# Issuing the late stores of a gated block-sparse and LoRA kernel from GpSimd's DMA queue instead of ScalarE's

## The chip, the cores and the metric

The kernel runs on one core of one Trainium2 chip. The metric is device time in microseconds (us), the median of several runs; lower is better.

## The reference

The input `x` has two batches of 1024 tokens with 1024 features. Every token is layer-normalised. Two products of 1024 by 1024 are taken of the result and combined with the input:

```
xn = layernorm(x)
s  = xn @ (weight masked in 32x32 blocks).T + bias
c  = softmax(((mean of xn over tokens) @ Wq.T) @ keys.T / sqrt(128))    # 8 numbers per batch
W  = W_org + sum over e of c[e] * lora_down[e] @ lora_up[e]             # folded, per batch
out = x + s * silu(xn @ W.T)
```

The kernel uses that the LoRA branch is linear: it folds the eight experts into one weight matrix per batch, which needs the coefficients `c` of that batch first. Everything is float32; each operand of a product is split into a high part (`fp32r`) and a low rest, and each product is three matmuls (high-high, high-low, low-high).

## The kernel before

**Stages.** Batch 0 is computed tile by tile: 128 tokens by 512 output columns per PSUM tile, 24 matmuls each (`gemm`, lines 425 to 427). The stages that matter here, with their place in the profiled span:

- about 100 to 155 us, `jobs_b`: the y product of batch 0 for the first 512 columns. Each tile's result is finished by `final_evac` in a tile `res` and queued for storing. Beside it the statistics of batch 1 are taken (GpSimd computes eight `rstd` by a power, line 152).
- about 155 to 206 us, `jobs_c`: the y product for the other 512 columns. Beside it VectorE normalises batch 1 in transposed form and forms, for each of four slices `j`, seven token sums (`wide_a`, `wide_b`, the operands of a seven-product scheme for batch 1), which are queued for storing in a DRAM tile `xv` (five stores for each j: `ac`, `bd`, and three single tiles). At the end the coefficients of batch 1 are computed: scores on TensorE (line 332), a few small VectorE operations (L334 to L337), the exponential `ex` on GpSimd (L339), the softmax's rest on VectorE (L345 to L352), and `scale_up` scales `up` by them (ScalarE L367, VectorE L368) into four tiles `cut`.
- about 204 to 300 us, the folding: sixteen calls of `fold`, one for each piece of 128 rows by 512 columns of batch 1's folded weight, between the eight tiles of batch 0's last product (`s_tile`). They come in bursts of 4, 4, 3, 3 and 2 folds. A fold loads `ds` and `wo`, splits `ds` into `dhi` and `dlo` (L380, L381), runs 12 matmuls (L389 to L391) with `cut`, adds `wo` (L396) and queues the sum for storing in a DRAM tile `yu`. After eight folds `scale_up(1, 1)` loads the other half of `up` (tiles `us`) and scales it for the last eight.
- from about 306 us, batch 1's seven products (L1127), which read `xv` and `yu` back. They store their results from SyncE and are not touched.

**Queued stores.** Late stores aren't issued where their data is produced. They are appended to a list, and `store_late` issues what has gathered there at fixed points of the program. There are 52 in all: 16 of batch 0's results (256 KB each), 20 of `xv` (8 of 512 KB and 12 of 256 KB), 16 of `yu` (256 KB each, in DRAM pieces of 512 bytes).

**Order.** TensorE, VectorE, ScalarE and GpSimd run in the order of the program (`manual_schedule`). The order on SyncE, which issues all the loads, is chosen by a planner that simulates the program. A store's instruction waits, in its engine's queue, until its data is there, and what stands behind it in that queue waits too.

**Buffers.** `ds`, `wo`, `us` and others take turns in one pool of six buffers (tag `st`), so that a load can wait for an earlier store of the same buffer to land. In the program, the third and the fourth load of `us` for the second half are in buffers that the stores of fold 5 and fold 6 (counted from 0) must leave first.

**Descriptors.** The program is built with a small area for descriptors that GpSimd would write: `dynamic_dma_scratch_size=SCRATCH`, and `SCRATCH = 1024` (bytes of each partition).

Of the kernel before, what the change touches and what calls it, by code (L numbers as in the profile page):

```python
# [32 lines left out]
def kernel(  # L33
# [26 lines left out]
    nc = tc.nc  # L60
# [414 lines left out]
    late_stores = []  # L475

    def store_late():

        while late_stores:
            nc.scalar.dma_start(*late_stores.pop(0))  # L480

    pending = []

# [119 lines left out]
    with tc.manual_schedule(engines={mybir.EngineType.PE, mybir.EngineType.DVE, mybir.EngineType.Activation, mybir.EngineType.Pool}):  # L603
# [233 lines left out]
        def jobs_b(i):  # L837
            if i == 0:
                yield J(scale_up, 0, 1)
            yield J(mix_jobs, y01, 0, 1, i)  # L840
            yield J(store_late)
            if i < 4:
                yield J(mask_part, 2 + i // 2, i % 2)
            for t in ((0,), (1, 2), (3, 4), (5,), (6, 7), (), (), ())[i]:
                yield J(nat_stats, 1, t)
            if i == 4:
                yield J(wide_load, 0, 0)
                yield J(wide_load, 0, 1)
            if i == 5:
                yield J(spread_stats)  # L850
                yield J(wide_a, 0)
            if i == 6:
                yield J(wide_b, 0)
            if i == 7:
                yield J(wide_load, 1, 0)
                yield J(wide_load, 1, 1)
# [76 lines left out]
        def jobs_c(i):  # L933
            yield J(s_mul, s1, 1, i)
            yield J(store_late)
            yield J(s_lo, s1, 1, i)
            if i in (1, 3):
                yield J(wide_load, (i + 3) // 2, 0)
                yield J(wide_load, (i + 3) // 2, 1)
            if i < 6:  # L940
                yield J((wide_a, wide_b)[i % 2], 1 + i // 2)
            if i == 6:
                yield steps[0]
                yield steps[1]
            if i == 7:
                yield steps[2]
                yield steps[3]
                yield J(scale_up, 1, 0)
# [6 lines left out]
        def fold(n):  # L955
            h, kt = folds[n]
            if n + 1 < len(folds):
                y_prep(1, *folds[n + 1])
            store_late()
            y_mul(1, h, kt)  # L960
            flush()
            y_sum(1, h, kt)
            ps, ws = staged.pop((1, h, kt))
            late_stores.append((
                yu[:, :, 2 * h + kt // 4, kt % 4, :].rearrange("u p n -> p u n"),
                ws.rearrange("p (u n) -> p u n", n=P),
            ))
            if n == NKT - 1:
                scale_up(1, 1)
# [297 lines left out]
```

## Time and profile before

| what | value |
|---|---|
| median of 3 runs | 461.96 us (461.96 to 462.08) |
| profiled execution | 463.29 us, span 461.2 us |
| TensorE busy | 443.0 us, 96% of the span, 2047 matmuls |
| VectorE, ScalarE, GpSimd busy | 313.0, 169.3, 37.9 us |
| SyncE's queue (q1) | 73.42 MB, 49.1% of the 16 DMA engines |
| ScalarE's queue (q10) | 15.73 MB, 10.1% |
| GpSimd's queue | no DMA in this profile |

All times below come from the one profiled execution, whose own time of 463.29 us is 1.33 us above the median. The span is what its records cover. "Idle before" and "releaser" say how long an engine stood still ahead of an instruction and which instruction ended that wait. The records of DMA-issuing instructions stand on a row of their own for each engine's queue (ACTq for ScalarE, SPq for SyncE); they aren't counted as busy, but the engine's later instructions come after them.

### The profile page before, as it was taken

Reading aid. Unit: us, or ns where it says so; the run is one execution under the profiler, and the core shown is the slowest. Engines: PE = TensorE matmul, PEld = TensorE weight load, DVE = VectorE, ACT = ScalarE, POOL = GpSimd, SP = SyncE. Lnnn points to the kernel's source line nnn. Section 1 sums busy time; section 2 is a strip of 40 time slices with the busy share of each in tenths; the row PEclk is TensorE's granted clock in tenths of the full one; section 3 lists DMA queues with packets and bytes.
Section 4 is the critical chain, followed back from the end, with each engine's and each line's share of the span. In section 5 each row is a group of like instructions: output and inputs, shape, how many; then the busy total and the mean of one; then the engine's idle time right before and its main releaser. Section 6 shows DMA issues by size and latency. Waiting matters only on the chain.

```text
span 461.2 us, 5714 instructions
## 1 busy us (share of the span) xinstructions
PE 443.0 (96%) x2047; PEld 362.6 (79%) x2047; DVE 313.0 (68%) x504; ACT 169.3 (37%) x277; POOL 37.9 (8%) x40
## 2 busy tenths in 40 slices
PE   7799999999999999996999899999999999999996
PEld 5689888888887888874887688877888888888884
DVE  6989877667775788846555776769496196467624
ACT  4676534363223222214224223158343432441510
POOL 3884210000100000001000000000000000000000
PEclk9999999999999999998999999999999999999999
DMA  8996317687952688797887985664264134207003
GB/s 286 391 343 212 114 42 231 179 274 258 294 207 92 199 316 287 257 299 235 256 248 250 279 278 159 222 192 156 85 171 141 54 120 155 91 28 223 23 1 114
DMA packets 48172, 89.52 MB, mean 194 GB/s; under 512 B 4752, under 2 KB 14992, under 8 KB 48144
## 3 DMA queue, kind: packets, MB, share of 16 engines
q1 hardware_dynamic: 34512, 73.42, 49.1%
q10 hardware_dynamic: 13632, 15.73, 10.1%
q8 instruction: 16, 0.26, 0.2%
q14 instruction: 12, 0.10, 0.1%
HBM read 69.21 MB, written 19.92 MB: 193 GB/s over the span
## 4 chain that ended last, share of the span: by engine, by line
PE 74%; DVE 11%; DMA 10%; ACT 3%; issue 2%; SPq 0%; DVEq 0%; ACTq 0%
PE acc_ps L1127 22%; PE py L1127 9%; PE acc_ps L425 8%; PE acc_ps L427 8%; PE acc_ps L426 8%; PE psw L391 6%; PE psw L389 6%; PE psw L390 6%; DMA ws<-in_wT_dram 3%; DMA xv<-bd 2%; DMA xs<-xv 2%; DVE slot L544 1%; DMA raw<-in_x_dram 1%; DMA yu<-wo 1%; DMA us<-in_up_dram 1%
## 5 line engine op out<-in xcount | busy, mean ns | idle before, releaser
L1127 PE MATMUL acc_ps<-xw,ow 128*128 128x512 f32 x480 | 113.8, 393 | 0.7 <-ACT acc_ps L1158 0.4
L426 PE MATMUL acc_ps<-slot,xgrp 128*128 128x512 f32 (+1 forms) x288 | 105.8, 367 | 2.7 <-DVE slot L544 2.7
L1127 PEld LDWEIGHTS acc_ps<-xw,ow 128*128 128x128 f32 x480 | 90.0, 188 | 21.7 <-ACT acc_ps L1158 0.8
L425 PE MATMUL acc_ps<-slot,xgrp 128*128 128x512 f32 (+1 forms) x288 | 106.6, 370 | 0.1
L427 PE MATMUL acc_ps<-slot,xgrp 128*128 128x512 f32 (+1 forms) x288 | 105.6, 367 | 0.7 <-DVE xgrp L556 0.7
L426 PEld LDWEIGHTS acc_ps<-slot,xgrp 128*128 128x128 f32 x288 | 54.3, 189 | 12.2 <-DVE slot L544 3.6
L427 PEld LDWEIGHTS acc_ps<-slot,xgrp 128*128 128x128 f32 x288 | 54.2, 188 | 10.2 <-DVE xgrp L556 1.1
L425 PEld LDWEIGHTS acc_ps<-slot,xgrp 128*128 128x128 f32 x288 | 54.3, 188 | 9.1 <-DVE stash L439 0.3
L389 PE MATMUL psw<-cut,dhi 128*128 128x512 f32 x128 | 50.9, 398 | 4.5 <-ACT dhi L380 4.3
L391 PE MATMUL psw<-cut,dlo 128*128 128x512 f32 x128 | 50.9, 398 | 1.6 <-DVE dlo L381 1.5
L390 PE MATMUL psw<-cut,dhi 128*128 128x512 f32 x128 | 50.6, 395 | 0.0
L1127 PE MATMUL py<-xw,ow 128*128 128x512 f32 x192 | 46.9, 392 | 0.0
L1127 PEld LDWEIGHTS py<-xw,ow 128*128 128x128 f32 x192 | 36.1, 188 | 8.1
L1031 DVE TENSOR_TENSOR ow<-raw,ow 128x1024 fp32r<-128x1024 f32 (+1 forms) x32 | 34.5, 1089 | 11.2 <-ACT ow L1030 11.2
L380 ACT CAST dhi<-ds 128x512 fp32r<-128x512 f32 x32 | 19.8, 618 | 43.1 <-PE psw L390 24.3
L396 DVE TENSOR_TENSOR wo<-wo,psw 128x512 f32<-128x512 f32 x32 | 22.0, 686 | 17.3 <-PE psw L391 17.2
L389 PEld LDWEIGHTS psw<-cut,dhi 128*128 128x128 f32 x128 | 24.3, 190 | 10.2 <-ACT dhi L380 4.7
L391 PEld LDWEIGHTS psw<-cut,dlo 128*128 128x128 f32 x128 | 24.4, 191 | 8.4 <-DVE dlo L381 3.2
L1030 ACT CAST ow<-raw 128x1024 fp32r<-128x1024 f32 (+1 forms) x32 | 29.3, 939 | 2.0 <-DVE xw L986 2.0
L390 PEld LDWEIGHTS psw<-cut,dhi 128*128 128x128 f32 x128 | 24.3, 190 | 5.7 <-DVE cut L368 0.5
L381 DVE TENSOR_TENSOR dlo<-ds,dhi 128x512 fp32r<-128x512 f32 x32 | 21.9, 686 | 8.0 <-ACT dhi L380 8.0
L1172 DVE TENSOR_TENSOR py<-py,s 128x512 f32<-128x512 f32 x8 | 5.6, 699 | 29.6 <-ACT s L1134 29.4
(151 smaller groups left out, 451.6 us busy)
## 6 DMA issues: line engine op xcount, KB each, us to landing
ds<-in_down_dram SPq DMA_DIRECT2D x32, 256.0 KB, 3.7
wo<-in_worgT_dram SPq DMA_DIRECT2D x32, 256.0 KB, 3.9
raw<-in_x_dram SPq DMA_DIRECT2D x11, 512.0 KB, 6.3
res<-in_x_dram SPq DMA_DIRECT2D x16, 256.0 KB, 3.7
us<-in_up_dram SPq DMA_DIRECT2D x16, 256.0 KB, 3.6
out_dram<-res ACTq DMA_DIRECT2D x16, 256.0 KB, 3.6
raw<-in_wu_dram SPq DMA_DIRECT2D x8, 512.0 KB, 5.0
yu<-wo ACTq DMA_DIRECT2D x16, 256.0 KB, 4.0
```

Of the source, the lines that this page charges most:

```text
L380: nc.scalar.copy(dhi, ds)
L381: nc.vector.tensor_tensor(dlo, ds, dhi.bitcast(F32), ALU.subtract)
L389: nc.tensor.matmul(ps, lhsT=dhi[:, c, :], rhs=u[c][:, 0, :], start=c == 0, stop=False)
L390: nc.tensor.matmul(ps, lhsT=dhi[:, c, :], rhs=u[c][:, 1, :], start=False, stop=False)
L391: nc.tensor.matmul(ps, lhsT=dlo[:, c, :], rhs=u[c][:, 0, :], start=False, stop=c == 3)
L396: nc.vector.tensor_tensor(ws, ws, ps, ALU.add)
L425: nc.tensor.matmul(ps, lhsT=xs[:, kt, 0, cols], rhs=w[:, kt, 0, wc], start=kt == 0, stop=False)
L426: nc.tensor.matmul(ps, lhsT=xs[:, kt, 0, cols], rhs=w[:, kt, 1, wc], start=False, stop=False)
L427: nc.tensor.matmul(ps, lhsT=xs[:, kt, 1, cols], rhs=w[:, kt, 0, wc], start=False, stop=kt == NKT - 1)
L1030: nc.scalar.copy(o[:, a:b, 0], raw[:, a:b])
L1031: nc.vector.tensor_tensor(o[:, a:b, 1], raw[:, a:b], o[:, a:b, 0].bitcast(F32), ALU.subtract)
L1127: nc.tensor.matmul(ps, lhsT=o[:, a, wl, j, :], rhs=xw[j][:, m, xl, :], start=start and j == 0 and k == 0, stop=j == 3 and k == 2, skip_gro ...
```

## The change

All 52 late stores are issued from GpSimd's queue. The diff is one line:

```diff
     def store_late():
 
         while late_stores:
-            nc.scalar.dma_start(*late_stores.pop(0))
+            nc.gpsimd.dma_start(*late_stores.pop(0))
```

The order of instructions on TensorE and VectorE stays as it was, and so does that of ScalarE's computing instructions. On GpSimd the stores now stand between the eight `rstd` powers and around the second `ex`: the 20 stores of `xv` come ahead of it, the 16 of `yu` behind it. The planner chooses a slightly different order of the loads on SyncE (two loads of the mask some places earlier, a few loads of the folding stage exchanged with their neighbours). The completion counters that SyncE's and ScalarE's DMAs took turns in are left to SyncE's; GpSimd's stores have eight of their own.

## The prediction

> **What bounds the kernel now.** I read the page first. TensorE is busy for 443.0 of 461.2 us, so a change of queue can only work in the 18 us in which TensorE stands still. The table of windows of 10 us shows where these are after the start-up (columns: window, length, busy us and count on PE, PEld, DVE, ACT, POOL, granted clock, DMA share, GB/s):
>
> ```profile
> PE 443.0 (96%) x2047; PEld 362.6 (79%) x2047; DVE 313.0 (68%) x504; ACT 169.3 (37%) x277; POOL 37.9 (8%) x40
> ```
>
> ```profile
> 200.00:210.00 10.00, 9.29 (x41) 7.09 (x39) 4.69 (x13) 1.82 (x3) 1.65 (x1) 1.00 0.92 312
> 210.00:220.00 10.00, 6.11 (x19) 4.41 (x20) 7.93 (x15) 5.01 (x9) 0.00 (x0) 0.83 0.65 211
> 250.00:260.00 10.00, 8.24 (x33) 5.57 (x32) 9.69 (x14) 4.25 (x8) 0.00 (x0) 1.00 0.84 261
> 215.00:217.50 2.50, 2.50 (x6) 2.02 (x7) 1.67 (x3) 0.62 (x1) 0.00 (x0) 0.50 0.94 270
> ```
>
> From 70 to 300 us every other window has at least 9.67 us of PE, but for 250 to 260 (8.24). So two places count: **the start of the folding** near 210 us and **the second half's scales** near 250 us. The timeline of ScalarE shows what precedes the first:
>
> ```profile
> 200.63 0.62 ACT L277 CAST slot<-ws 128x512 fp32r<-128x512 f32 x1 [8.32 <-DVE ws L274]
> ...
> 201.00 1.18 ACTq L480 DMA_DIRECT2D xv<-bd  x1
> 202.22 1.70 ACTq L480 DMA_DIRECT2D xv<-tt  x2
> 203.96 1.65 ACTq L480 DMA_DIRECT2D xv<-xt  x1
> 205.66 0.69 ACT L448 ACTIVATE stash<-acc_ps,rstd 128x512 f32<-128x512 f32 x1 [4.41 <-DMA xv<-bd]
> 206.24 0.61 ACT L277 CAST slot<-ws 128x512 fp32r<-128x512 f32 x1
> 210.77 2.56 ACT L367 ACTIVATE cut<-us,c 128x512 fp32r<-128x512 f32 x4 [3.92 <-DVE c L352]
> ```
>
> The five stores of the last `xv` group hold ScalarE until 205.61. VectorE's L282 waits for L277 (206.89), its `sc` stands behind that (207.49), then `ex`, `c`, four `cut`, `dhi`, and TensorE at last:
>
> ```profile
> 208.19 1.65 POOL L339 TENSOR_TENSOR ex<-ebase,sc 128x8 f32<-128x8 f32 x1 [74.19 <-DVE sc L337]
> ```
>
> ```profile
> 213.89 0.61 PE L389 MATMUL psw<-cut,dhi 128*128 128x512 f32 x1 [4.29 <-ACT dhi L380]
> ```
>
> The second place is in the chain of waits from 238 to 258 us:
>
> ```profile
> 240.57 0.70 DVE wo L396
> ...
> 241.29 4.12 DMA yu<-wo
> 245.41 0.02 issue
> 245.43 3.97 DMA us<-in_up_dram
> 249.40 0.02 issue
> ...
> 249.48 0.73 ACT cut L367
> 250.22 0.03 issue
> 250.24 0.57 DVE cut L368
> ```
>
> The store of fold 6 frees the buffer of the fourth `us`. Fold 8's matmuls already run from 248.54, and the ones of the fourth `cut` start at 250.62 with pauses of 0.2 us: no slack.
>
> **What the skill says.** "DMA: Bandwidth & Descriptors", Specifications: first byte about 1 us on GpSimd's path, 0.6 us on ScalarE's; an estimate of +0.4 us per store. No DMA of the trace before comes from GpSimd, so nothing here shows it. The same page, Terms and "SWDGE vs HWDGE vs iDMA": GpSimd writes descriptors of 16 bytes into rings in an SBUF area, 16 partitions for each direction. With this kernel's 1024 bytes per partition, that is an estimate of 1024 / 16 x 16 / 16 = 64 descriptors for each of 16 DMA engines. An `xv` or result store has 8 rows for each engine, so 9 with the completion; a `yu` store has 8 x 4 pieces of 512 bytes, so 33. Two `yu` stores (66) don't fit at once. "SBUF - State Buffer", the box on DVE blocking DMA: VectorE's two-port modes keep GpSimd from writing descriptors, while float32 tensor-tensor work doesn't; nearly all of VectorE's late work is that, so I add nothing. "TensorE: Matmul & The Clock Gate", Part 1: after an idle window of about 3.4 us the clock halves. The trace agrees: clock 0.50 after the 4.29 us gap, 1.00 after one of 1.54 us at 257.24.
>
> **The change, part by part.** R is a fold's L396 ending, L its store landing.
>
> *Removed from ScalarE: 52 issues.* Near 205 us: tile 7's matmuls end near 203.4, so L448 can start at 203.6, L277 at 204.2 (its input is ready at 204.12), L282 0.65 later, `sc` 0.6 later: 205.5 instead of 207.5. The rest (`ex` 1.65, small operations, 4 `cut`, `dhi`) keeps its length; `ds` is loaded once L282 frees its buffer, so it moves along. TensorE's gap falls by 1.9 us from 4.29 to 2.4. That is under the window, so the slow clock goes too: from 213.89 to 220 TensorE ran 19 matmuls where 6.11 / 0.227 = 27 fit, 8 x 0.227 = 1.8 us. **Gain 3.7 us.** Elsewhere ScalarE's issues delay nothing of TensorE: zero, with ScalarE idle for 63% as cover.
>
> *Added to GpSimd: 52 issues of about 1 us.* Sixteen result stores and eight `rstd` share 100 to 150 us. The last `rstd` ended at 133.45, its reader (L873) starts at 140.2: 6 us of cover for at most 1 us, zero. Ahead of `ex` stand the last five `xv` stores. Their data is ready at 196.3, so at 1 us each they are done at 201.3, and `ex` wants GpSimd at 206.2: 5 us of cover, zero. Storing earlier than ScalarE did (data of the third group ready at 184.4, issued at 186.2) only lets loads start earlier.
>
> *Moved: the `yu` stores past each other.* From ScalarE they were in flight together; issue to landing took 2.5, 5.8, 3.8, 2.5, 2.5, 5.5, 4.1 us for folds 0 to 6, issued 0, 2.74, 5.46, 8.18, 16.39, 19.11, 21.83 us after fold 0's. With room for one, each waits for the one ahead. I take +0.5 us each (0.4 and a poll of the ring). L0 = 3.0, L1 = 3.0 + 6.3 = 9.3, L2 = 13.6, L3 = 16.6, L4 = 19.6, L5 = 25.6, L6 = 30.2. Before, L6 was 21.83 + 4.1 = 25.9. The fourth `us`, its `cut` and fold 8 are 4.3 us late with no slack; the third (1.0 us late) has about 1.2. A gap over 4.3 us halves the clock again, 1.8 us. **Loss 6.1 us.** The loads behind in SyncE's queue: `ds` of fold 7 waits for L2, lands 3.7 us later at 17.7, wanted at 19.8 (its matmuls start at 21.1, split 1.3 before); `ds` of fold 8 for L3, with 7 us to spare; fold 10's for L7, which moves with fold 8: zero. Later bursts (3, 3, 2) leave 13.7 us for three stores of 4.3: no backlog.
>
> *SyncE's changed order and counters:* fewer shared counters can only take waits away; TensorE waits for no load from 70 to 140 us: zero. Read-back of `yu` starts at 288 and ends with the last store; at +0.5 us it has 8 us before its readers.
>
> **Sum:** -3.7 + 6.1 = +2.4 us on the profiled 463.29 (465.7), and as a shift on the median: 461.96 + 2.4 = **464.4 us**. The unknown is the added time per store. At 0: L6 = 28.7, 2.8 us late, gap short enough for the clock: -0.9. At 1.0 us: 7.8 late, +5.9. So 461.1 to 467.9 for this case itself. A measurement here tells about 0.2%, 0.9 us, from no change.
>
> **Rivals.** (1) *The ring holds several `yu` stores.* Then fold 6's store is 0.5 us late, and -3.7 + 0.5 = -3.2: 458.8, faster. For it: no view shows the ring; against it: 66 against 64. It decides from 31 descriptors or fewer per store and engine. (2) *GpSimd itself is late with `ex`*: at over (206.2 - 196.3) / 5 = 2 us per store `ex` waits. At 3 us `ex` starts at 211.3, TensorE at 217.0: the first gain turns into +3.1, with the loss of 6.1 it makes 471.2. Against it: 1 us per store in the skill. (3) *Gain and loss cancel*: at +0.2 us per store fold 8 is 3.2 us late with a full clock, -0.5: 461.5.
>
> **Chances.** The serial case 0.68 (of it slower 0.45, within 0.2% 0.13, faster 0.10), (1) 0.20 (faster 0.18, same 0.02), (2) 0.07, (3) 0.05. Faster 0.28, same 0.20, slower 0.52. The range takes in (1) and the serial case with up to 1.2 us per store (9.2 late, +7.3): 458.6 to 469.3.
>
> **What would show it.** Right: the gap before the first L389 at about 2.4 us with full clock; stores of folds 1 to 6 landing one after another, never two in flight; a gap of about 4 us inside fold 8, released by ScalarE's or VectorE's `cut`. Wrong: `yu` stores overlapping; a first gap of over 4 us with `ex` behind a store; TensorE waiting in the tile stages before 200 us.

## The result, and the profile after

The changed kernel takes 469.13 us in the median of 4 runs beside 462.02 us for 4 runs of the kernel before, 7.1 us more. The ratio on record is 1.0113 with an interval of 1.0069 to 1.0156, less than the quotient of these medians (1.0154); the record does not show how it comes out of these eight runs. Measured a second time (the run after_again below) the medians are 468.40 and 463.92 us and the ratio is 1.0093 (1.0060 to 1.0127). So the changed kernel is slower, by 1 to 1.5% or 4 to 7 us. The ratios leave out executions more than 1.5% above the fastest of their kernel and the medians keep them, so a ratio need not be the quotient of two medians.

The profiled execution took 470.25 us, the longest of the four; its span is 468.5 us. The page of the kernel after, first the busy time of the engines, then the queue that the stores now use (packets, MB, share of the 16 DMA engines):

```profile
PE 449.0 (96%) x2047; PEld 366.7 (78%) x2047; DVE 313.1 (67%) x504; ACT 168.7 (36%) x277; POOL 70.0 (15%) x92
q0 software_dynamic: 4672, 15.73, 9.2%
```

The 15.73 MB have left ScalarE's queue for GpSimd's. TensorE runs the same 2047 matmuls and is busy 6.0 us longer, while its idle time has grown only from 18.2 to 19.5 us. The mean granted clock of the profile fell from 0.995 to 0.982, and (1 - 0.982) x 468.5 - (1 - 0.995) x 461.2 = 6.1 us is an estimate of the time that the lower clock costs. It matches the 6.0, so most of the span's 7.3 us is lower clock. The table of windows of the kernel after shows where (columns as in the one of before; the last three are granted clock, DMA share and GB/s):

```profile
210.00:220.00 10.00, 8.45 (x29) 6.22 (x28) 6.63 (x11) 4.32 (x8) 1.38 (x2) 0.83 0.62 214
240.00:250.00 10.00, 8.47 (x37) 6.38 (x35) 2.30 (x5) 1.34 (x2) 1.38 (x2) 1.00 0.71 236
250.00:260.00 10.00, 6.54 (x13) 3.48 (x14) 4.28 (x7) 3.71 (x6) 1.51 (x2) 0.71 0.49 171
260.00:270.00 10.00, 10.00 (x36) 7.97 (x36) 9.57 (x14) 2.48 (x5) 2.05 (x3) 0.78 0.90 271
```

From 250 to 260 us TensorE gets 13 matmuls done where the kernel before did 33, and from 260 to 270 it is busy throughout but at 0.78 of its clock.

**The start of the folding** came earlier, as the timeline of the kernel after shows (start, length, engine, line, operation, and in brackets the idle time before it and its releaser):

```profile
205.78 1.67 POOL L339 TENSOR_TENSOR ex<-ebase,sc 128x8 f32<-128x8 f32 x1 [4.72 <-DVE sc L337]
208.38 2.56 ACT L367 ACTIVATE cut<-us,c 128x512 fp32r<-128x512 f32 x4 [4.04 <-DVE c L352]
212.15 0.51 PE L389 MATMUL psw<-cut,dhi 128*128 128x512 f32 x1 [1.55 <-ACT dhi L380]
```

Up to `cut` that chain is 2.4 us earlier than before (`ex` stood at 208.19, `cut` at 210.77). Then ScalarE waits 0.53 us for the load of `ds`, so the first fold starts 1.74 us earlier (212.15 against 213.89). TensorE's gap is 1.55 us instead of 4.29; it shrank by more than 1.74 because the matmuls ahead of it end 1.0 us later (210.60 against 209.60). Yet the window of 210 to 220 us has the same clock of 0.83 as before.

**The yu stores** are the GpSimd records of L480 in the timeline of the kernel after:

```profile
218.89 0.77 POOL L480 DMA_DIRECT2D yu<-wo  x1
222.00 0.76 POOL L480 DMA_DIRECT2D yu<-wo  x1 [2.35 <-DVE dlo L381]
228.31 0.75 POOL L480 DMA_DIRECT2D yu<-wo  x1 [5.54 <-DVE wo L396]
...
239.88 0.75 POOL L480 DMA_DIRECT2D yu<-wo  x1 [3.61 <-issue]
245.34 0.76 POOL L480 DMA_DIRECT2D yu<-wo  x1 [4.72 <-issue]
250.12 0.75 POOL L480 DMA_DIRECT2D yu<-wo  x1 [4.01 <-issue]
```

The releasers are of no use here: no instruction of the program ends this wait, so the profile names whatever came last, or "issue". What tells is the landing of the store ahead. The stores take 2.8, 6.0, 6.3, 4.6, 5.1, 4.5 and 3.1 us from start to landing, and each starts some 0.3 us after the one ahead has landed: two are never in flight. Fold 6's sum was ready at 240.92 and its store started 9.2 us later. The later stores (folds 9 to 15) wait in the same way, but TensorE is busy for all of the 40 us from 270 to 310 us, so no cost of theirs shows.

**Fold 8** then has no operand. SyncE issues the four loads of `us` later than before and over a longer time (first the kernel before, then after):

```profile
239.77 5.98 SPq L364 DMA_DIRECT2D us<-in_up_dram  x4
```

```profile
245.46 8.13 SPq L364 DMA_DIRECT2D us<-in_up_dram  x4
```

The chain of waits of the kernel after:

```profile
250.12 3.13 DMA yu<-wo
253.24 0.02 issue
253.26 3.79 DMA us<-in_up_dram
...
257.13 0.73 ACT cut L367
```

and TensorE's gaps inside fold 8, from the timeline:

```profile
249.93 0.49 PE L389 MATMUL psw<-cut,dhi 128*128 128x512 f32 x1 [1.53 <-ACT cut L367]
...
257.91 0.80 PE L389 MATMUL psw<-cut,dhi 128*128 128x512 f32 x1 [3.04 <-ACT cut L367]
```

The store of fold 6 lands at 253.25, the fourth `us` at 257.05 (249.40 before), and fold 8, split by gaps, runs its last matmuls at half clock (0.80 us for the first one after the gap, against 0.49 at full clock).

### The profile page after: what moved, and what is told of

Its sections match the earlier page's. It is cut to its first block, busy times and chain, and to the rows that moved or that the text cites. A ratio compares the mean times of both kernels' runs of the same rounds, so it can differ in the third digit from the quotient of the medians.

```text
span 468.5 us, 5745 instructions
## 1 busy us (share of the span) xinstructions
PE 449.0 (96%) x2047; PEld 366.7 (78%) x2047; DVE 313.1 (67%) x504; ACT 168.7 (36%) x277; POOL 70.0 (15%) x92
## 3 DMA queue, kind: packets, MB, share of 16 engines
q0 software_dynamic: 4672, 15.73, 9.2%
## 4 chain that ended last, share of the span: by engine, by line
PE 70%; issue 12%; DVE 8%; DMA 4%; POOL 3%; ACT 1%; SPq 0%; POOLq 0%; DVEq 0%; ACTq 0%
PE acc_ps L1127 22%; PE py L1127 9%; PE acc_ps L425 8%; PE acc_ps L427 8%; PE acc_ps L426 8%; PE psw L389 5%; PE psw L390 5%; PE psw L391 5%; DVE slot L544 1%; DMA raw<-in_x_dram 1%; DMA ws<-in_wT_dram 1%; POOL xv L480 1%; POOL yu L480 1%; DMA us<-in_up_dram 1%; DVE ramp L535 1%
## 5 line engine op out<-in xcount | busy, mean ns | idle before, releaser
L427 PEld LDWEIGHTS acc_ps<-slot,xgrp 128*128 128x128 f32 x288 | 54.8, 190 | 10.2 <-DVE xgrp L556 1.1
L389 PE MATMUL psw<-cut,dhi 128*128 128x512 f32 x128 | 53.1, 415 | 7.0 <-ACT cut L367 4.6
L390 PE MATMUL psw<-cut,dhi 128*128 128x512 f32 x128 | 52.5, 410 | 0.3 <-DVE cut L368 0.3
L391 PE MATMUL psw<-cut,dlo 128*128 128x512 f32 x128 | 52.3, 408 | 0.0
L389 PEld LDWEIGHTS psw<-cut,dhi 128*128 128x128 f32 x128 | 25.2, 197 | 14.7 <-ACT cut L367 6.3
L390 PEld LDWEIGHTS psw<-cut,dhi 128*128 128x128 f32 x128 | 25.3, 198 | 7.2 <-DVE cut L368 1.9
L396 DVE TENSOR_TENSOR wo<-wo,psw 128x512 f32<-128x512 f32 x32 | 21.9, 685 | 13.0 <-PE psw L391 12.9
L391 PEld LDWEIGHTS psw<-cut,dlo 128*128 128x128 f32 x128 | 25.5, 199 | 6.4 <-DVE dlo L381 0.9
```

Of the source, the lines that this page charges most:

```text
L389: nc.tensor.matmul(ps, lhsT=dhi[:, c, :], rhs=u[c][:, 0, :], start=c == 0, stop=False)
L390: nc.tensor.matmul(ps, lhsT=dhi[:, c, :], rhs=u[c][:, 1, :], start=False, stop=False)
L391: nc.tensor.matmul(ps, lhsT=dlo[:, c, :], rhs=u[c][:, 0, :], start=False, stop=c == 3)
L396: nc.vector.tensor_tensor(ws, ws, ps, ALU.add)
L427: nc.tensor.matmul(ps, lhsT=xs[:, kt, 1, cols], rhs=w[:, kt, 0, wc], start=False, stop=kt == NKT - 1)
```

## The experiments

The theory: GpSimd's descriptor area has room for one `yu` store only, and the wait for room delays the loads that need these buffers. The rivals: such a store is slow on this queue by itself; or GpSimd is late for another reason. All ratios below that of after are to the kernel before on the same chip. "SyncE's waits" is the time from 212 to 262 us that SyncE's queue stood at loads (L364, L375, L377; two lines less in ring96 and ring64) until a `yu` store had landed, added up from the list of waits. SyncE issues its loads in the same order of tiles in after, ring96, ring64, yu_flat and yu_56; it differs from that in 4 places in yu_act, 2 in yu_mix and 23 in the kernel before. So among the first five the planner's order is no rival.

| run | yu stores | ratio (interval) | median, before, us | SyncE's waits, us |
|---|---|---|---|---|
| before | ScalarE | 1 | | 14.2 |
| after | GpSimd | 1.0113 (1.0069 to 1.0156) | 469.13, 462.02 | 24.4 |
| after_again | GpSimd | 1.0093 (1.0060 to 1.0127) | 468.40, 463.92 | 22.5 |
| yu_act | ScalarE | 0.9981 (0.9959 to 1.0003) | 461.94, 462.47 | 10.2 |
| yu_pool | GpSimd | 1.0132 (1.0093 to 1.0171) | 468.33, 462.47 | 26.0 |
| ring96 | GpSimd, area 1536 | 1.0000 (0.9974 to 1.0025) | 462.49, 462.47 | 10.1 |
| ring64 | GpSimd, area 1024 | 1.0109 (1.0073 to 1.0146) | 467.94, 462.47 | 21.3 |
| yu_flat | GpSimd, 2 KB runs | 0.9918 (0.9887 to 0.9949) | 460.52, 464.39 | 10.4 |
| yu_flat_act | ScalarE, 2 KB runs | 0.9994 (0.9974 to 1.0015) | 463.86, 464.39 | 12.9 |
| yu_mix | alternately | 0.9974 (0.9950 to 0.9998) | 462.17, 463.92 | 7.8 |
| yu_56 | folds 5, 6 on ScalarE | 1.0074 (1.0050 to 1.0098) | 465.18, 461.82 | 15.6 |

**Which stores make the loss.** yu_act sends only the `yu` stores back to ScalarE; yu_pool sends only these to GpSimd. Each queued store carries its queue:

```diff
# yu_act (yu_pool has the two queues exchanged)
-            nc.gpsimd.dma_start(*late_stores.pop(0))
+            (lambda d, s, q=nc.gpsimd: q.dma_start(d, s))(*late_stores.pop(0))
...
-                ws.rearrange("p (u n) -> p u n", n=P),
+                ws.rearrange("p (u n) -> p u n", n=P), nc.scalar,
```

> The 16 stores of yu go back to ScalarE's queue; the xv and result stores stay on GpSimd. If the loss comes from yu stores waiting for each other in GpSimd's ring, it goes, and the gain at the start of the folding stays: 460.0 us (458.5 to 461.5), the gap before the first L389 about 1.6 us, no gap over 1 us near the fourth cut. If GpSimd's path as such is slow, for the other 36 stores too, it stays near 467 to 469 us.

> Only the 16 yu stores are on GpSimd's queue; the xv and result stores are back on ScalarE. If the yu stores cause the loss: the loss of the whole change without its gain, 469 to 472 us, fold 6's store landing some 8 us after its data is ready. If the other stores cause it: 462 us.

Measured: 0.9981 and 1.0132, 6.4 us between the two medians. The sixteen `yu` stores make the whole loss; the other 36 on GpSimd show no cost. yu_act's 461.94 us lies above the range expected (458.5 to 461.5) and its first gap is 2.59 us, not 1.6: the loss went, but a gain over the kernel before is not shown (the interval reaches 1.0003). TensorE's gap before the first fold is 3.33 us in yu_pool and 2.59 in yu_act; it is 4.29 and 4.71 in the two profiles with all stores on ScalarE (before and yu_flat_act) and at most 2.59 wherever the `xv` stores are on GpSimd. So the gap shrinks mostly by moving these.

**Room, or the queue itself.** ring96 gives the area 1536 bytes of each partition. The 512 bytes come from `inv_s`, a matrix of 1/1024: `ones_r` takes its place in the token sums, and the factor goes into the scores, so nothing is left out. ring64 has the same edit but keeps 1024 bytes.

```diff
# ring96 (ring64: the same with SCRATCH = 1024)
-    inv_s = c0pool.tile([P, P], F32R, name="inv_s")
-    nc.vector.memset(inv_s.bitcast(F32), 1.0 / S)
...
-                    nc.tensor.matmul(mp, lhsT=inv_s, rhs=hi[:, h, :], start=True, stop=False)
-                    nc.tensor.matmul(mp, lhsT=inv_s, rhs=lo[:, h, :], start=False, stop=True)
+                    nc.tensor.matmul(mp, lhsT=ones_r, rhs=hi[:, h, :], start=True, stop=False)
+                    nc.tensor.matmul(mp, lhsT=ones_r, rhs=lo[:, h, :], start=False, stop=True)
...
-            nc.vector.tensor_scalar(sc, sp, (1.0 if b == 0 else 1.0 / S) / math.sqrt(KQ), None, ALU.mult)
+            nc.vector.tensor_scalar(sc, sp, 1.0 / S / math.sqrt(KQ), None, ALU.mult)
...
-SCRATCH = 1024
+SCRATCH = 1536
```

> All late stores on GpSimd as in the change, with SCRATCH 1536 in place of 1024, an estimate of 96 descriptors for each DMA engine, room for two yu stores (66) and a result (9). The space comes from dropping the tile inv_s (ones_r is used, and the scale moves into the scores). If the ring's room is the cause: yu stores in pairs in flight, fold 6's store landing about 26 us after fold 0's issue as before, 460 to 462 us. If each store is only slow by itself or GpSimd issues one at a time whatever the room: same as with 1024, 467 to 470 us.

> Control of the one with 1536: the same dropping of inv_s, SCRATCH left at 1024. Both theories: as the changed kernel, 467 to 470 us, yu stores strictly one after another.

Measured: 1.0000 and 1.0109, 5.5 us between two kernels that differ in one number. The timeline of ring96, the first four stores (its lines are two less):

```profile
219.05 0.78 POOL L478 DMA_DIRECT2D yu<-wo  x1
221.70 0.76 POOL L478 DMA_DIRECT2D yu<-wo  x1 [1.86 <-DVE wo L394]
224.44 0.75 POOL L478 DMA_DIRECT2D yu<-wo  x1 [1.99 <-DVE wo L394]
228.23 0.76 POOL L478 DMA_DIRECT2D yu<-wo  x1 [3.05 <-DVE wo L394]
```

and of ring64:

```profile
217.45 0.77 POOL L478 DMA_DIRECT2D yu<-wo  x1
220.56 0.76 POOL L478 DMA_DIRECT2D yu<-wo  x1 [2.34 <-DVE dlo L379]
226.73 0.75 POOL L478 DMA_DIRECT2D yu<-wo  x1 [5.41 <-DVE wo L394]
231.43 0.76 POOL L478 DMA_DIRECT2D yu<-wo  x1 [3.96 <-DVE res L470]
```

With more room the stores start 2.65, 2.74 and 3.79 us apart, each 0.4 to 0.5 us after its fold's sum is ready, and two are in flight; with 1024 bytes 3.11, 6.17 and 4.70. The instruction is as long in both (0.75 us), and SyncE's order is the same. So the wait is for room in this area.

**Fewer pieces instead of more room.** yu_flat keeps 1024 bytes and lays `yu` out so that each of a store's 128 rows is one run of 2 KB instead of four of 512 bytes. Its later reads come in 512 byte pieces. yu_flat_act has the same layout with all late stores on ScalarE.

```diff
# yu_flat; yu_flat_act is this on the kernel before
-        yu = dram.tile([4, P, 4, 4, P], F32, name="yu")
+        yu = dram.tile([P, 4, 4, 4, P], F32, name="yu")
...
-                yu[:, :, 2 * h + kt // 4, kt % 4, :].rearrange("u p n -> p u n"),
+                yu[:, 2 * h + kt // 4, kt % 4, :, :],
...
-            src = wu[p] if kind == "s" else yu[p].rearrange("p a j n -> p (a j n)")
-            c = slice(2 * i * NH, 2 * (i + 1) * NH)
-            nc.sync.dma_start(raw_flat[:, c], src[:, c])
+            src = wu[p].rearrange("p (a j n) -> p a j n", a=4, j=4) if kind == "s" else yu[:, :, :, p, :]
+            c = slice(2 * i, 2 * (i + 1))
+            nc.sync.dma_start(raw[:, c], src[:, c])
```

> All late stores on GpSimd as in the changed kernel, SCRATCH 1024 as there, but yu is laid out in DRAM as [P, 4, 4, 4, P], so that each of a store's 128 rows is one run of 2 KB instead of four runs of 512 B; the reads in the state loop then come in 512 B pieces. Ring theory: a store needs a quarter or so of the descriptors, several fit into the ring, the stores start when their data is ready (about 2.7 to 3 us after the store before where the folds are back to back), the fourth us is loaded before 250, fold 8 has no gap of 3 us, and the time is 460 to 463.5 us like ring96. Rival (yu stores on this queue are served one at a time whatever their descriptors): starts stay 4.3 to 6 us apart and the time is 466 to 470 us. If the 512 B reads cost the state loop something, yu_flat_act shows it too.

> The kernel before (all late stores on ScalarE) with the same layout of yu as yu_flat: the control for the layout alone. Ring theory: within 1.5 us of the kernel before, 460.5 to 463.5 us, and within 1.5 us of yu_flat. Rival: 4 us or more below yu_flat.

Measured: 0.9918 and 0.9994. The layout alone shows no change, and on GpSimd it is 3.3 us faster than on ScalarE (460.52 against 463.86), where at most 1.5 was expected: with the wait gone, the change that was slower becomes a gain. The record lists the span and the mean granted clock of every execution, so span x (1 - clock) estimates the time that each lost to a low clock. In the mean that is 1.3 us for yu_flat (6 executions) and 4.6 us for yu_flat_act (14), so nearly all of this gain is clock. The timeline of yu_flat:

```profile
217.16 0.54 POOL L480 DMA_DIRECT2D yu<-wo  x1
218.34 0.54 POOL L480 DMA_DIRECT2D yu<-wo  x1 [0.64 <-DVE wo L396]
221.08 0.54 POOL L480 DMA_DIRECT2D yu<-wo  x1 [2.21 <-DVE wo L396]
```

GpSimd's part of a store fell from 0.75 to 0.54 us, and the second starts 1.18 us after the first, in flight with it (these stores take 2.3 to 6.0 us to land, median 4.0). The page counts 4672 packets for this queue as it did for the kernel after, so its packets don't show how full the area is.

**Half of the stores.** yu_mix leaves layout and area as changed and sends every second `yu` store to ScalarE. Against yu_act:

```diff
-                ws.rearrange("p (u n) -> p u n", n=P), nc.scalar,
+                ws.rearrange("p (u n) -> p u n", n=P), (nc.scalar if kt % 2 else nc.gpsimd),
```

> All late stores on GpSimd except every second yu store, which goes to ScalarE; layout and SCRATCH as in the changed kernel. A GpSimd yu store then has two folds' time, about 5.5 us, for the one before it to land. Ring theory: of the first four the two on GpSimd seldom wait (landing 2.8 to 6 us), the fourth us is loaded by about 248 to 252, fold 8 loses nothing or less than 1 us, and the time is within 1.5 us of yu_act, 460 to 463.5 us on a chip where the kernel before shows 462 to 464. Rival (software queue slows each yu store by itself, or its stores wait on GpSimd's other work): half of the loss stays, 464.5 to 467 us.

Measured: 0.9974, as the room theory has it, with 7.8 us the least of SyncE's waits. Stores of the same kind on the same queue show no loss when each has two folds' time.

**Two stores, a miss.** If the loss came only through the buffers that the stores of folds 5 and 6 free, moving these two would be enough. Against yu_act:

```diff
-                ws.rearrange("p (u n) -> p u n", n=P), nc.scalar,
+                ws.rearrange("p (u n) -> p u n", n=P), (nc.scalar if n in (5, 6) else nc.gpsimd),
```

> The changed kernel, but the yu stores of folds 5 and 6 alone go to ScalarE; the other 50 late stores stay on GpSimd, with the same layout and SCRATCH. If the loss comes by way of the third and fourth us, which need the buffers of these two stores, then it goes although fourteen yu stores still wait for each other: the fourth us is loaded by 246 to 250, fold 8 has no gap over 1 us, and the ratio to the kernel before is 0.996 to 1.001 (yu_act: 0.998). Rival (the loss is spread over all folds whose stores wait): a ratio of 1.006 to 1.010, with gaps elsewhere or a still late us behind folds 3 and 4.

Measured: 1.0074, the rival's figure. The timeline of yu_56, ScalarE and its queue first, then TensorE:

```profile
235.64 0.62 ACT L380 CAST dhi<-ds 128x512 fp32r<-128x512 f32 x1 [3.28 <-DMA ds<-in_down_dram]
235.72 0.38 ACTq L480 DMA_DIRECT2D yu<-wo  x1
241.79 0.62 ACT L380 CAST dhi<-ds 128x512 fp32r<-128x512 f32 x1 [5.53 <-DMA ds<-in_down_dram]
241.87 0.37 ACTq L480 DMA_DIRECT2D yu<-wo  x1
```

```profile
248.27 0.50 PE L389 MATMUL psw<-cut,dhi 128*128 128x512 f32 x1 [3.22 <-ACT cut L367]
```

The gap in fold 8 is still there. Fold 6's sum was ready at 237.58, but its store stands behind the split of fold 8's `ds` in ScalarE's queue and went out at 241.87. And that `ds` was late because SyncE issues in order. In the list of waits of SyncE's queue, 226 to 246 us (engine, line, what it waited for, total, times, longest):

```profile
SPq L377 <- DMA yu<-wo: 12.3, 3, 4.2
```

It stood three times at a load of `wo` whose buffer a GpSimd `yu` store had yet to leave, and all loads behind it stood too. So the stores of folds 0 to 4 delay fold 8 as well, by way of SyncE's queue: the first load of `us` goes out at 242.82 here. In the kernel after, L377 adds 13.7 us to this against 5.9 before.

**The clock.** The two warm kernels put matmuls on ones (result unused) between the first state tile and the first fold, to fill TensorE's gap: ten in yu_act, eighteen in the kernel before, eight in yu_flat.

```diff
             s_tile(i)
+            if i == 0:
+                hot = ps_s.tile([P, 4, P], F32, name="hot", tag="ps_s")
+                for _ in range(18):
+                    nc.tensor.matmul(hot, lhsT=ones_r, rhs=ones_r.unsqueeze(1).to_broadcast([P, 4, P]), start=True, stop=True)
```

> yu stores on ScalarE, the others on GpSimd, plus ten matmuls on ones (128x512, result unused) between the first state tile and the first fold, which fill TensorE's gap there. If the low clock at 213 to 220 follows from the gap, it is at full clock in every execution and the time falls below yu_act by up to 1.8 us where yu_act had lost it: 459 to 461.5 us. If a gap there decides nothing, the time is yu_act's, 461.5 to 462.5 us.

> The kernel before, all late stores on ScalarE, plus eighteen such matmuls in the same place. The fold still starts when dhi is there (about 213.9), but the matmuls behind it should run at full clock: by the estimate of the prediction 1.8 us less than the kernel before, about 460.2 us; no change (461.8 to 462.5 us) if the clock falls for another reason or if the loss was hidden by folds that wait for us.

> yu_flat plus eight matmuls on ones (result unused) between the first state tile and the first fold. Its profile had no low clock at 210 to 220 behind a gap of 1.57 us, where the changed kernel had one behind 1.55 us. If such a loss falls in some executions of yu_flat, filling the gap takes it out: 0.3 to 1.5 us below yu_flat's ratio of 0.992, a ratio of 0.989 to 0.991. If not, the ratio stays at 0.992, or rises by up to 0.001 where the dummies delay the first fold.

Measured: yu_act_warm 0.9933 (0.9902 to 0.9963), before_warm 0.9977 (0.9958 to 0.9996), yu_flat_warm 0.9915 (0.9890 to 0.9941). The table of windows of before_warm:

```profile
210.00:220.00 10.00, 9.17 (x40) 6.96 (x39) 7.71 (x13) 6.04 (x10) 0.00 (x0) 1.00 0.71 226
```

Filling the kernel before's gap of 4.29 us took the low clock away (1.00 for 0.83), worth 1.1 us in the median (463.33 against 464.39), under the estimate of 1.8. By the clock of every execution the time lost fell by just that, from 4.1 us (36 executions) to 2.3 (22), but some of it came back elsewhere. yu_act_warm stands 0.5% below yu_act, though on another chip. In yu_flat_warm no gain over yu_flat shows (0.9915 and 0.9918, on two chips). The warm kernels are no part of the change; yu_flat, at 0.9918, is the simplest version that beats both kernels, by 3.9 us on the kernel before's median.

**The change again.**

> The changed kernel as it is, again, beside the next two on one chip. If the loss is a property of the kernel and not of the executions seen so far, 1.0 to 1.5% over the kernel before (466 to 470 us where that shows 462 to 464), with yu stores that start one after another, 4 to 6 us apart, and a gap of 2 to 3 us in fold 8. If its profile is one of the quicker starts, half of what its first profile lost beyond the forecast (the clock in the first 40 us and at 213 to 216 us) is gone.

Measured: 1.0093. Its profile (span 466.9 us) has the same stores and the same fold 8 (gap of 3.30 us), but full clock from 210 to 220 us behind a gap of 2.25 us.

## Why the prediction was right, and what it mis-sized

The forecast was 464.4 us and slower, by 2.4 us. The sign and the mechanism held: stores that wait for each other, and a late fold 8. The size did not: the medians differ by 7.1 us and, measured again, by 4.5. The 469.13 us lie outside the 461.1 to 467.9 given for this case itself and only 0.2 us under the upper end of the whole range, which was drawn for 1.2 us more per store.

- **"Moved: the yu stores past each other."** Confirmed: ring96 against ring64 and yu_flat against the kernel after show the wait for room, and no other cost on GpSimd was seen. The estimate from the Trainium skill ("DMA: Bandwidth & Descriptors", Terms and "SWDGE vs HWDGE vs iDMA") of 64 places for two stores of 33 fits: at 1536 bytes, an estimate of 96 places, two fit. A store without room waits until the one ahead has landed, as the 0.3 us between a landing and the next start show. Rival (1), several stores in the area, is ring96 and yu_flat, and for yu_flat its figure of 3.2 us gained is what yu_flat against yu_flat_act measured (3.3). ring96, at 1.0000, did not show that gain. Its 14 executions lost 3.6 us each to a low clock in the mean, as the kernel before did on that chip (3.3), and those of yu_flat 1.3; that is 2.3 of the 3.8 us between their ratios. Why yu_flat meets the low clock less often isn't settled.
- **"I take +0.5 us each"** is a term that was mis-sized. L6 was 250.12 + 3.13 - 218.89 = 34.4 us after fold 0's store, not 30.2; in the three other profiles with all `yu` stores on GpSimd and 1024 bytes it was 32.0 (after_again), 31.5 (ring64) and 31.1 (yu_pool). Over the 26.7 us of seven transfers from ScalarE that is 1.1, 0.75, 0.7 and 0.6 us each. About 0.3 of it stands in every trace, the time between a landing and the next start. That a transfer itself is slower from GpSimd isn't shown: from start to landing the seven took 32.4, 30.1, 29.6 and 29.3 us there, and from ScalarE 26.1 to 31.7 in before, yu_act, before_warm and yu_act_warm. With 0.6 to 1.1 the prediction's own sum gives +3.3 to +6.6, close to the 4.5 and 7.1 measured; but that is in part luck, as the next points show.
- **"ds of fold 8 for L3, with 7 us to spare"** looked at each load's own buffer. yu_56 shows the path that this missed: a `wo` load that waits for an earlier store holds every load behind it in SyncE's queue.
- **"Removed from ScalarE"**: the first fold started 1.74 us earlier, near the 1.9 forecast, though part of the reason was wrong: `ds`, said to move along, came 0.53 us late. **"That is under the window, so the slow clock goes too"** failed in the profiled execution and held in after_again, where the gap is 2.25 us. The clock there isn't a function of the gap's length: see below.
- **"A gap over 4.3 us halves the clock again, 1.8 us"** is the other term that was mis-sized: there was no such gap. There were gaps of 0.78 us ahead of fold 7 and of 1.53, 0.29 and 3.04 us in fold 8, 5.6 in all, and the clock was low twice. (1 - 0.71) x 10 + (1 - 0.78) x 10 = 5.1 us in the profile of after, and (1 - 0.66) x 10 = 3.4 in 250 to 260 us of after_again: two to three times the 1.8.
- **"Added to GpSimd"**: right. A store of `xv` or a result holds GpSimd for 0.54 us, a `yu` store for 0.75, below the 1 us taken (the page's 1 us is the time to the first byte), and `ex` waits for `sc`, not for a store. Rival (2) is out. The `yu` stores are within 0.02 us of each other (0.75 to 0.77), so no delay by VectorE's work shows, as assumed.
- **"Later bursts (3, 3, 2) leave 13.7 us for three stores of 4.3: no backlog"** was wrong without a cost that shows: every store of folds 9 to 15 started 0.3 us after the one ahead had landed, and the last landed at 300.0 us (291.0 before).

The sum for the two profiled executions: the first gap -2.7, these gaps +3.9 (5.6 against 0.18 and 1.54 around the same place before), fold 8's clock +5.1, the clock at 210 to 220 us 0. That is +6.3. Another 1.6 us is hardly an effect of the change: from 0 to 40 us the clock is 0.96 in this profile and 1.00 in that of before, and it is 0.96 in yu_act and 1.00 in yu_flat, ahead of the first late store. It made the matmuls before the first fold late, so 1.0 us of the 2.7 above is probably its doing. The 7.9 compare with 7.3 in the spans; the clocks are rounded to a hundredth, 0.05 us in each window of 10 us and 0.2 in the one of 40. Over all executions on record the low clock cost 6.8 us in after (4) and in after_again (7), against 3.8 for the kernel before beside after_again (39): so an estimate of 3.0 of the 4.4 us between the means of the last two is low clock.

## What to carry to other kernels

In this kernel the DMAs moved to GpSimd's queue shared a small descriptor area. Before you move a store there, count a store's contiguous pieces for each DMA engine against it, and if two stores don't fit, make the pieces longer or the area larger, or leave every second one where it was. When stores free buffers for loads that one queue issues in order, follow the whole queue, not only the load that needs the buffer. And look at TensorE's busy time beside its idle time: here most of the loss was the same matmuls at half clock behind short gaps.

## What the runs showed of the hardware that was not expected

The clock can halve behind a short gap. The Trainium skill ("TensorE: Matmul & The Clock Gate", Part 1) names an idle window of about 3.4 us and calls it free-running. The traces agree with the window and its running by itself, but not with "idle". In the eleven profiles with more than one change of the clock, every change lies a whole number of times 3.413 us after the others. In the kernel after, half clock begins at 18.58, 213.14, 250.69 and 257.52 us: 57, 11 and 2 times 3.413 us apart. Where this grid lies in the span differs between executions. So a trace can be cut into the grid's own windows, here around the first gap of after and of yu_flat (where the one change, at 456.89 us, gives the grid):

```profile
209.73:213.14 3.41, 1.86 (x7) 0.94 (x6) 2.85 (x5) 2.42 (x4) 0.00 (x0) 1.00 0.50 178
213.14:216.56 3.42, 3.42 (x9) 2.68 (x9) 1.52 (x3) 0.62 (x1) 0.00 (x0) 0.50 0.86 299
```

```profile
207.72:211.14 3.42, 1.85 (x8) 1.24 (x7) 3.08 (x5) 2.87 (x6) 0.00 (x0) 1.00 0.43 121
211.14:214.55 3.41, 3.41 (x15) 2.47 (x14) 1.51 (x3) 0.83 (x2) 0.00 (x0) 1.00 0.87 274
```

The busy share is TensorE's in the grid window that holds most of the gap (two are given where a large part lies in each):

| gap before the first L389, us | busy share | clock in the next window | run |
|---|---|---|---|
| 1.55 | 0.55 | 0.50 | after |
| 1.57 | 0.54 | 1.00 | yu_flat |
| 1.69 | 0.51 | 0.50 | ring96 |
| 1.96 | 0.46 | 1.00 | yu_56 |
| 2.04 | 0.67, 0.66 | 1.00 | ring64 |
| 2.25 | 0.58 | 1.00 | after_again |
| 2.44 | 0.50 | 1.00 | yu_mix |
| 2.59 | 0.58, 0.66 | 1.00 | yu_act |
| 3.33 | 0.43, then 0.50 | 1.00, then 0.50 | yu_pool |
| 4.29 | 0.07 | 0.50 | before |
| 4.71 | 0.06 | 0.50 | yu_flat_act |

Half clock lasted one or two windows, and each window of it is 0.5 x 3.41 = 1.7 us. Over all fourteen traces, without their first 7 and last 12 us, the clock fell 18 times. All 9 windows at full clock in which TensorE was busy for less than 0.43 were followed by half clock, none of the 1756 at 0.58 or more was, and of the 26 between 9 were and 17 were not. So it seems to matter how much of one window a gap takes: the 2.59 us of yu_act, shared by two windows, did no harm, and the 1.55 us in one window of after did. What decides between 0.43 and 0.58 stays open: after and yu_flat differ by 0.01 there and had different outcomes, the busy share is modelled, and no run set the phase of the grid.
